# A second Strassen step in all seven products of layer 1's q and V

## The chip, the cores and the metric

The kernel runs on one core of one Trainium2 chip. The metric is the device time of one execution, in microseconds. The time before is 2786.17 us, the median of 3 runs (2785.94 to 2787.55).

A core has a TensorE (PE: matrix products, which it writes into PSUM), a VectorE (DVE), a ScalarE (ACT), a GpSimd (POOL) and a SyncE (SP, which issues transfers). Each works through its own instructions in order and waits on semaphores for the others. In this kernel a tile of PSUM is two banks of 512 fp32 columns by 128 partitions.

## The reference

Eight images of 512 channels by 32 x 32 positions pass through two attention layers, in fp32.

```python
# layer 0, 8 heads
h = group_norm(x, norm_w, norm_b)                  # 32 groups
qkv = einsum('oc,bchw->bohw', qkv_w, h) + qkv_b    # q, k, v by head
attn = softmax(einsum('bhnd,bhmd->bhnm', q, k) / sqrt(64))
x = x + proj_w @ (attn v) + proj_b
# layer 1, one head, statistics over the whole image
n = (x - mean(x)) * rsqrt(var(x) + eps) * gn_gamma + gn_beta
q, k, v = wq n + bq, wk n + bk, wv n + bv
attn = softmax(einsum('bci,bcj->bij', q, k) * 512 ** -0.5)
out = x + wo (einsum('bcj,bij->bci', v, attn)) + bo
```

## The kernel before

Layer 1's products are folded once, ahead of the images: q becomes one product with wq and wk together, whose partner in the scores is the image itself, and V one product with wv and wo together. The images are then worked on one after another. For image b the program runs layer 0's scores and values (`layer0`), then for image b+1, ahead of time, layer 0's V, its even pairs of heads (`qk02`), for image b the projection, for image b+1 the odd pairs (`qk13`), and then layer 1 of image b (`attention1`): q, V, scores, values.

**Strassen.** A product of 512 x 512 by 512 x 1024 is cut into quarters and computed as seven products of quarters instead of eight (the Winograd form): A11 B11, A12 B21, S1 T1, S2 T2, S3 T3, S4 B22 and A22 T4, where S1 to S4 are sums of quarters of A, and T1 to T4 of B. Some of these seven are cut again in the same way, which is called "twice" in the names. `pair` in `by_two_steps` (L614) does two such products side by side, in seven steps: both products' results share one bank, the left and the right half. Four of the seven products get the second step before the change (`PAIRS`); A11 B11, S2 T2 and S3 T3 (the "line") do not, in q, in V and elsewhere.

**q** (`make_q`, L1518) runs 12 products of 512 columns and 28 of 256. **V** (`make_v_twice`, L972) runs 56 of 128 columns and 24 of 256. ACT copies a sum that comes first into its place, DVE adds the later ones.

**Second-step operands.** What the second step needs is prepared: for the weights, sums of their quarters are made once, kept in DRAM, and fetched for each image on ACT's queue (`WeightTwice`, L556). For the image, `Ready.halve` makes them on GpSimd during `qk13` (`quarters_b`, L545; its instructions are at L535 and L541), four parts: B21, B22, T1, T4.

**Order.** PE's, ACT's and DVE's instructions stay in the order in which the program emits them. A product is a generator that yields after each step, and `at_steps` (L680) calls the hooks listed for a step's number between its steps, so a dictionary such as `hooks_v` says what DVE, ACT and GpSimd are given where. `together` (L668) interleaves generators. GpSimd's and SP's instructions are placed by the framework's scheduler.

**Buffers.** There are 36 SBUF tiles of 128 x 1024 in the pool "t", three weight tiles in "w", and in PSUM two tiles each of the tags "s" and "o" (two banks each, eight banks in all). A tile is taken over by the next request of its tag, which waits until everything that used it is done.

**Statistics.** Layer 1's mean and variance come from sums that ACT makes (`moments`, L335, two passes per 128 x 512 piece), which small GpSimd operations join (L350 to L356). A matmul with `in_sample` (L305) averages over the partitions and puts its result into the unused second bank of a product's PSUM tile (the list `spares`), DVE reduces it (L307), and then GpSimd (L363 to L367) and a second such matmul do the variance. Layer 0's statistics of image b+2 are made by the same means during image b's V: the image is loaded again for it, at q's step 3, in four pieces of 512 KB.

**q's combinations.** S1 to S4 of q for the scores (`finish_q`, by `finish`, L187; instructions at L195) and the second step's sums of S1 (`halve_a`, L518) are DVE work between V's steps.

**Kept.** The odd pairs' q and k go to DRAM after `qk13` (`Kept`, L921) and are fetched during layer 1's values; the even pairs' stay in SBUF.

## Time and profile before

| | |
|---|---|
| median of 3 runs | 2786.17 us |
| the profiled execution | 2786.2 us |
| its span | 2784.5 us |
| PE busy | 2777.8 us (100%) |
| DVE busy | 2117.3 us (76%) |
| ACT busy | 1178.1 us (42%) |
| GpSimd busy | 500.9 us (18%) |
| DMA, HBM over the span | 106 GB/s |

The span is that of the instructions on the core; the execution's own time is 1.7 us longer. Busy shares are of the span. A line of the timeline has the start in microseconds from the span's start, the length, the engine, the line of the kernel, the operation, output and input by the program's names, the shape, how many instructions in a row it stands for, and in brackets the idle time before and what ended it. PE's matmuls are pipelined, so the length of a group includes its last one's drain; the distance from start to start tells the pace.

### The profile page before, as it was taken

The numbers are of one execution on the slowest core, as the hardware profiler recorded it, in microseconds if no ns is written. First come the engines' busy times: TensorE is split into PE (matmuls) and PEld (weight loads), VectorE is DVE, ScalarE is ACT, GpSimd is POOL, SyncE is SP. The second block draws the span as 40 slices with busy tenths as digits, with TensorE's granted clock in tenths as the row PEclk, the third lists the DMA queues.
The fourth block names the chain that finished last, engine by engine and source line by source line (L and its number), as shares of the span: only waits on it lengthen the run. The fifth ranks groups of instructions, "written<-read, shape, count | busy, mean of one in ns | idle before, by whom it ended". The sixth has DMA issues, their size and how long they took to land.

```text
span 2784.5 us, 41074 instructions
## 1 busy us (share of the span) xinstructions
PE 2777.8 (100%) x16192; PEld 1620.0 (58%) x16192; DVE 2117.3 (76%) x2929; ACT 1178.1 (42%) x1883; POOL 500.9 (18%) x535
## 2 busy tenths in 40 slices
PE   9999999999999999999999999999999999999999
PEld 5437664377643776447764477645676356753375
DVE  6787677876788767887678775877758877688877
ACT  3462433625346153462525524265342643226622
POOL 0001240012400124002140031400413004220121
PEclk9999999999999999999999999999999999999999
DMA  7545513254132541325313253222533235131001
GB/s 258 193 119 171 185 57 111 58 182 170 57 110 58 185 168 65 107 62 201 144 65 107 77 201 129 89 90 74 196 129 110 69 102 197 69 140 32 23 16 39
DMA packets 103433, 321.32 MB, mean 115 GB/s; under 512 B 23820, under 2 KB 24620, under 8 KB 96832
## 3 DMA queue, kind: packets, MB, share of 16 engines
q1 hardware_dynamic: 81072, 268.75, 28.6%
q10 hardware_dynamic: 22160, 49.87, 5.4%
q8 instruction: 129, 2.11, 0.3%
q14 instruction: 72, 0.59, 0.1%
HBM read 231.01 MB, written 63.74 MB: 106 GB/s over the span
## 4 chain that ended last, share of the span: by engine, by line
PE 99%; DVE 0%; ACT 0%; issue 0%; POOL 0%; ACTq 0%; POOLq 0%
PE ps_o L1110 16%; PE s L1061 16%; PE ps_o L1867 10%; PE ps_l_v L708 6%; PE ps_l_qk L959 5%; PE ps_l L1701 5%; PE ps_s L1684 4%; PE ps_s_v L980 4%; PE ps_s L1701 4%; PE ps_s_qk L952 3%; PE ps_l_q L693 3%; PE ps_o_v L980 3%; PE ps_o_qk L952 3%; PE ps_l_p L693 3%; PE ps_s_q L1540 2%; PE ps_f_q L1540 2%
## 5 line engine op out<-in xcount | busy, mean ns | idle before, releaser
L865 ACT ACTIVATE p<-s 128x1024 f32<-128x1024 f32 x505 | 516.7, 1025 | 308.6 <-PE s L1061 301.4
L867 DVE TENSOR_TENSOR acc<-acc,p 128x1024 f32<-128x1024 f32 x384 | 469.0, 1221 | 63.4 <-ACT p L865 55.0
L1110 PE MATMUL ps_o<-p,v_back 64*64 64x512 f32 x3528 | 455.3, 589 | 0.0
L1110 PEld LDWEIGHTS ps_o<-p,v_back 64*64 64x64 f32 x3528 | 134.9, 133 | 243.6 <-issue 240.1
L1061 PE MATMUL s<-qk_back,qk_back 64*64 64x512 f32 x1792 | 233.0, 590 | 0.0
L1061 PE MATMUL s<-c_q,c_k 64*64 64x512 f32 x1736 | 224.4, 590 | 0.0
L535 POOL TENSOR_TENSOR B_twice_p<-o 128x512 f32<-128x512 f32 x14 | 20.9, 1494 | 1065.6 <-DMA kept_v<-c_v 607.9
L1867 PE MATMUL ps_o<-t_p,s_v 128*128 128x512 f32 x384 | 169.6, 596 | 0.0
L1061 PEld LDWEIGHTS s<-qk_back,qk_back 64*64 64x64 f32 x1792 | 67.7, 133 | 126.3 <-issue 113.0
L1061 PEld LDWEIGHTS s<-c_q,c_k 64*64 64x64 f32 x1736 | 64.9, 133 | 119.3 <-issue 103.2
L1675 ACT ACTIVATE p<-p,factor 128x512 f32<-128x512 f32 (+1 forms) x112 | 84.6, 780 | 114.8 <-DVE p L1711 87.9
L1867 PEld LDWEIGHTS ps_o<-t_p,s_v 128*128 128x128 f32 x384 | 71.8, 190 | 88.4 <-issue 88.0
L1711 DVE TENSOR_TENSOR p<-ps_l,p 128x512 f32<-128x512 f32 x136 | 90.8, 686 | 41.0 <-PE ps_l L1701 39.7
L644 DVE TENSOR_TENSOR c_v<-ps_l_v,c_v 128x512 f32<-128x512 f32 x120 | 80.0, 688 | 54.6 <-PE ps_l_v L708 54.4
L1689 ACT COPY p<-ps_s 128x512 f32<-128x512 f32 x96 | 53.1, 588 | 141.5 <-PE ps_s L1684 141.5
L867 DVE TENSOR_TENSOR acc<-p,p 128x1024 f32<-128x1024 f32 x57 | 69.7, 1222 | 47.8 <-ACT p L865 47.7
L1711 DVE TENSOR_TENSOR p<-ps_s,p 128x512 f32<-128x512 f32 x112 | 74.8, 685 | 36.6 <-PE ps_s L1701 21.7
L959 PE MATMUL ps_l_qk<-t,w_qk 128*128 128x512 f32 x224 | 98.4, 592 | 0.0
L626 ACT COPY c_q<-ps_s_qk 128x512 f32<-128x512 f32 x56 | 32.7, 584 | 138.8 <-PE ps_s_qk L952 138.8
L626 ACT COPY c_v<-ps_s_v 128x512 f32<-128x512 f32 x90 | 52.0, 585 | 86.8 <-PE ps_s_v L980 86.8
L535 POOL TENSOR_TENSOR B_twice<-x 128x512 f32<-128x512 f32 x16 | 20.1, 1277 | 373.7 <-PE ps_s_qk L952 196.6
L1672 POOL TENSOR_TENSOR acc<-acc,p 128x512 f32<-128x512 f32 x48 | 83.6, 1741 | 13.6 <-ACT p L1675 11.1
(579 smaller groups left out, 5703.7 us busy)
## 6 DMA issues: line engine op xcount, KB each, us to landing
x<-in_x SPq DMA_DIRECT2D x88, 512.0 KB, 10.3
w_qk<-stored_qk SPq DMA_DIRECT2D x14, 1792.0 KB, 9.2
fold<-acc SPq DMA_DIRECT2D x56, 256.0 KB, 4.0
qk_twice<-stored_qk_twice ACTq DMA_DIRECT2D x28, 512.0 KB, 3.9
kept_v<-c_v SPq DMA_DIRECT2D x28, 512.0 KB, 3.9
w_wqk<-stored_wqk SPq DMA_DIRECT2D x8, 1792.0 KB, 7.0
w_wvo<-stored_wvo SPq DMA_DIRECT2D x8, 1792.0 KB
v_back<-kept_v SPq DMA_DIRECT2D x28, 512.0 KB, 5.6
```

The lines of the kernel that those rows point to most:

```text
L693: nc.tensor.matmul(bank, w[a][:, k, c * P : (c + 1) * P], bs[b][:, k, :], start=fresh and k == 0, stop=k == 1, skip_group_check=True,)
L708: nc.tensor.matmul(bank[:, u * 2 * P : (u + 1) * 2 * P], bs[b][:, k, n * P : (n + 1) * P], w[a][:, k, :], start=fresh and u == k == 0, sto ...
L865: nc.scalar.activation(p, s, AF.Exp, scale=factor)
L867: nc.vector.tensor_tensor(acc, first, p, ALU.add)
L952: nc.tensor.matmul(bank[:, i * 2 * P : (i + 1) * 2 * P], parts[a][x], twice_b[v][y], start=start and i == 0, stop=True, skip_group_check=True,
L959: nc.tensor.matmul(bank, of(i, a)[:, k, :], bs[v][:, k, :], start=start and k == 0, stop=k == 1, skip_group_check=True,)
L980: nc.tensor.matmul(bank[:, (2 * i + u) * P : (2 * i + u + 1) * P], twice_b[v][y][:, u * P : (u + 1) * P], parts[a][x], start=start and i = ...
L1061: nc.tensor.matmul(s[cols, j, :], ks[pair][k0 // HALF][rows, k0 % HALF : k0 % HALF + HD], qs[pair][g][rows, :], start=True, stop=True,)
L1110: nc.tensor.matmul(o[cols, half, :], vs[n][kt % 4 // 2][rows, h, c0 : c0 + HD], p[rows, j, :], start=kt == 0, stop=kt == NT - 1,)
L1701: nc.tensor.matmul(bank[:, u * 2 * P : (u + 1) * 2 * P], v[y][:, u * P : (u + 1) * P], a[x], start=start and u == 0, stop=True, skip_group ...
L1711: nc.vector.tensor_tensor(at(r, t), bank, at(r, t), ALU.add)
L1867: nc.tensor.matmul(bank, v_parts[kt // 2][a][:, kt % 2, c * P : (c + 1) * P], p_parts[kt // 2][b][:, kt % 2, cols], start=fresh and kt == ...
```

## The change

It applies to images 0 to 6; the last image keeps the former q and V.

1. q and V: all seven products take the second step, in `seven_by_two_steps`. The groups z (A11 B11 and S2 T2, two products a step) and w (S3 T3) run interleaved first; then c (S1 T1 and A22 T4) and d (A12 B21 and S4 B22). d adds its results onto z, all by DVE. After z and w, four additions on DVE combine them; after c's last step (`n == 11`) four more are written, and after those d's last two. q needs 49 products of 256 columns, V 98 of 128.
2. The twice-combined weights of q and V grow from two tiles to four (the last half filled). The new sums are made once, by GpSimd, during image 0's round.
3. `Ready.halve` makes seven parts instead of four on GpSimd during `qk13`: 21 operations instead of 12.
4. The averages of layer 1's norm use the spare bank of z's "o" tile.
5. q's S1 to S4 and S1's second-step sums go from DVE to GpSimd, all at V's step 0. `Norm.untaken` makes one more small vector, `c_up`.
6. The even pairs' q and k are kept in DRAM too, and fetched at the values' step 6.
7. The second load of x is written in two parts, and its eight moments are divided: four in q's steps 15 to 24, four in V's.

```diff
+    REST = [[("A11", "B11"), ("S2", "T2")], [("S3", "T3")]]
+    TWICE = {"wqk1": PAIRS + REST, "wvo1": PAIRS + REST}
+        def __init__(self, name):
+            self.pairs, self.tiles = TWICE.get(name, PAIRS), []
+            for n, pair in enumerate(self.pairs):
+                t = flat(tile2(f"{name}_twice_{n}"))[:, : len(pair) * HALF]
+                nc.scalar.dma_start(t, stored[f"{name}_twice"][:, n * N : n * N + t.shape[1]])
+                self.tiles.append(t)
...
+    def seven_by_two_steps(multiply, at, z, c, w, bias, name):
+        def group(tag, products, use_of):
+            line, single = (banks(t, f"ps_{t}{tag}_{name}") for t in "so")
+            spares.append(single[:, 1, :])
+            line, single = line[:, 0, :], single[:, 0, :]
+            for bank, x, y, start, fresh, r, t in [
+                (line, "A11", "B11", True, True, 0, 0), (single, "A12", "B21", True, False, 0, 0),
+                (line, "S2", "T2", False, True, 0, 1), (single, "S1", "T1", True, True, 1, 1),
+                (line, "S3", "T3", False, False, 1, 1), (single, "S4", "B22", False, False, 0, 1),
+                (line, "A22", "T4", False, True, 1, 0),
+            ]:
+                multiply(bank, products, x, y, start)
+                tiles, always = use_of
+                to = at(tiles, r, t)
+                of = bank[:, : len(products) * 2 * P].rearrange("p (i q) -> p i q", i=to.shape[1])
+                if fresh and not always:
+                    nc.scalar.copy(to, of)
+                else:
+                    nc.vector.tensor_tensor(to, of, to, ALU.add)
+                yield
+        def plus(to, x, y, by=None):
+            if by is None:
+                nc.vector.tensor_tensor(to, x, y, ALU.add)
+            else:
+                nc.vector.scalar_tensor_tensor(to, x, by, y, ALU.add, ALU.add)
+        yield from together(group("z", REST[0], (z, False)), group("w", REST[1], (w, False)))
+        for k in range(2):
+            plus(z[k][:, 1, :], z[k][:, 0, :], z[k][:, 1, :], bias and bias(k, 0))
+        for k in range(2):
+            plus(w[k], w[k], z[k][:, 1, :], bias and bias(k, 1))
+        one = group("c", [("S1", "T1"), ("A22", "T4")], (c, False))
+        two = group("d", [("A12", "B21"), ("S4", "B22")], (z, True))
+        spares.clear()
+        next(one)
+        yield
+        n = 0
+        for g in [one, two] * 6 + [two]:
+            next(g)
+            n += 1
+            if n == 11:
+                for k in [1, 0]:
+                    plus(z[k][:, 1, :], z[k][:, 1, :], c[k][:, 0, :])
+                    plus(c[k], c[k], w[k].unsqueeze(1).to_broadcast([P, 2, HALF]))
+            if n < 13:
+                yield
+        if bias:
+            for k in range(2):
+                nc.scalar.activation(z[k][:, 0, :], z[k][:, 0, :], AF.Identity, bias=bias(k, 0))
+        yield
+        spares.clear()
...
+        if b == 0:
+            steps = [s for name in ["wqk1", "wvo1"] for s in make_twice(name, range(2, 4), None, nc.gpsimd)]
...
-        put_qk(pairs, 0, to["qs"], to["ks"])
+        to["qk02"] = Kept(pairs, f"qk02_{b % 2}")
-        for n, part in [(1, "B21"), (1, "B22"), (2, "T1"), (8, "T4")]:
+        for n, part in [(1, "B11"), (1, "B21"), (4, "T2"), (6, "T3"), (8, "B22"), (8, "T1"), (8, "T4")]:
             hooks.setdefault(n, []).append(lambda part=part: ready.halve(part))
...
+            hooks = {
+                1: [norm.both_halves], 5: [norm.mean_of_all], 8: [norm.deviation], 12: [norm.untaken],
+                16: [lambda: twice_w.append(WeightTwice("wvo1"))],
+            }
+                hooks[0], hooks[10] = ([lambda i=i: load_later(i)] for i in range(2))
+                for n in range(4):
+                    hooks.setdefault(15 + 3 * n, []).append(lambda n=n: measure_later(n))
+                    hooks_v.setdefault(15 + 3 * n, []).append(lambda n=n: measure_later(n + 4))
+            at_steps(make_q_twice(w), hooks)
...
-        for n in range(1, 5):
-            hooks_v.setdefault(2 * n + 3, []).append(lambda n=n: finish_q(n))
-        hooks_v.setdefault(17 if last else 13, []).append(lambda: halve_a("S1"))
+            for n in range(1, 5):
+                hooks_v.setdefault(0, []).append(lambda n=n: finish_q(n, nc.gpsimd))
+            hooks_v[0].append(lambda: halve_a("S1", None, nc.gpsimd))
+            at_steps(make_v_all(w), hooks_v)
...
-                    10: [lambda: put_qk(to["qk"].back(), 1, qs, ks)],
+                    6: [lambda: put_qk(to["qk02"].back(), 0, qs, ks)],
+                    10: [lambda: put_qk(to["qk13"].back(), 1, qs, ks)],
```

`make_q_twice` and `make_v_all` supply the two products with `multiply`, one matmul of 256 columns per product and step in q and two of 128 in V, and with `at`, the place of a quarter's result. `Norm.untaken` gets `c_up`, the difference of two columns of `c`, as a bias for w.

## The prediction

> **What bounds the kernel now.** First the page: busy time by engine, then the chain that ended last.

> ```profile
> PE 2777.8 (100%) x16192; PEld 1620.0 (58%) x16192; DVE 2117.3 (76%) x2929; ACT 1178.1 (42%) x1883; POOL 500.9 (18%) x535
> ...
> PE 99%; DVE 0%; ACT 0%; issue 0%; POOL 0%; ACTq 0%; POOLq 0%
> ```

> TensorE never rests, so a product less is worth its whole time, and any new wait of TensorE costs its whole length: nothing is slack on PE. The other engines matter only where PE would wait for them. Next the timeline of PE around one image's q and V (image 2):

> ```profile
> 995.65 1.93 PE L693 MATMUL ps_l_q<-x,w_wqk 128*128 128x512 f32 x4
> 997.42 1.89 PE L1540 MATMUL ps_f_q<-x,w_wqk 128*128 128x256 f32 x8
> ...
> 1018.87 0.61 PE L980 MATMUL ps_s_v<-w_wvo,x 128*128 128x128 f32 x4
> 1019.32 0.61 PE L980 MATMUL ps_s_v<-w_wvo,t 128*128 128x128 f32 x4
> ...
> 1034.94 7.17 PE L708 MATMUL ps_l_v<-w_wvo,t 128*128 128x256 f32 x32
> 1041.95 1.88 PE L1684 MATMUL ps_s<-q,x 128*128 128x512 f32 x4
> ```

> q takes 1018.87 - 995.65 = 23.22 us, V 1041.95 - 1018.87 = 23.08. A matmul shows as two records. From start to start, one of 512 columns paces at 0.8625 us, of 256 at 0.4313 ((999.15 - 997.42)/4, 999.15 being the next group's start), of 128 at 0.2234 (0.447 for four records).

> Then ACT, DVE and GpSimd in the same stretch, since they empty PSUM and feed the averages:

> ```profile
> 1019.96 0.59 ACT L626 COPY c_v<-ps_s_v 128x512 f32<-128x512 f32 x1 [2.02 <-PE ps_s_v L980]
> 1021.34 0.63 ACT L333 ACTIVATE mean<-x 128x512 f32<-128x512 f32 x1
> ```
> ```profile
> 976.59 1.88 DVE L440 TENSOR_TENSOR t<-x,x 128x1024 f32<-128x1024 f32 x1
> 1006.31 0.69 DVE L1528 TENSOR_TENSOR c_q<-ps_f_q,c_q 128x512 f32<-128x512 f32 x1 [0.17 <-PE ps_f_q L1540]
> 1023.31 1.22 DVE L195 TENSOR_TENSOR s_q<-q,q 128x1024 f32<-128x1024 f32 x1
> 1033.60 0.69 DVE L649 TENSOR_TENSOR c_v<-c_v,c_v 128x512 f32<-128x512 f32 x1
> ```
> ```profile
> 974.88 2.51 POOL L535 TENSOR_TENSOR B_twice<-x 128x512 f32<-128x512 f32 x2 [28.09 <-PE ps_s_qk L952]
> 977.34 6.86 POOL L541 TENSOR_TENSOR B_twice<-x,B_twice 128x256 f32<-128x256 f32 x4
> 990.66 0.20 POOL L350 TENSOR_TENSOR part<-part,stat 128x4 f32<-128x4 f32 x1
> 1007.18 0.30 POOL L363 TENSOR_SCALAR spread<-stat,mean_m 128x4 f32<-128x4 f32 x1 [14.92 <-DVE mean_m L307]
> ```

> A copy out of PSUM starts about 0.2 us after its matmul's paced end and holds ACT 0.59 us; a DVE add from PSUM takes 0.69 (0.60 apart when back to back); an SBUF add of 1024 columns 1.22 (1.13 apart), of 512 0.69. GpSimd's 12 halving operations end at 990.66, far ahead of the mean.

> [...] the 1024-column add is 1.88 us at 976.59, beside GpSimd, and 1.22 alone. [...]

> **The change, part by part**, for each of the seven images that get it.

> *Products.* q before: 12 x 0.8625 + 28 x 0.4313 = 22.42. After: all seven products in seven parts each, 49 x 0.4313 = 21.13. V before: 56 x 0.2234 + 24 x 0.4313 = 22.86; after 98 x 0.2234 = 21.89. Gain on paper 1.29 + 0.97 = 2.26; against the measured stages, which hold 0.28 of averages and about 0.7 of small gaps, up to 3.0.

> *The seam from q to V.* Call E the end of q's first half (groups z, w). Then c and d run 14 pairs of matmuls x 0.8625 = 12.08. In DVE's written order, four additions (`n == 11`) stand before d's last two adds, and the first needs ACT's copy of c's last sum: PE ends it at E + 12 x 0.8625 = E+10.35, the copy runs E+10.55 to 11.15. Then DVE: 0.73 + 1.13 + 0.73 + 1.13 (512, 1024, 512, 1024 columns; each 1024 one waits for the one before), then 0.60 and 0.69: E+16.1. d's last bank is the very bank that V's second product (group w) takes. PE gets there after V's first product, 4 x 0.2234 = 0.89, at E+12.97. So PE waits 16.1 - 12.97 = **3.1 us**. Behind it in PE's order stand all of V's other products; nothing covers it. Before, V's groups of four records follow one another at 0.447 us without a gap. Bounds: 2.6 (each DVE operation at its back-to-back pitch, no gap) to 3.9 (ACT's copy late by 0.8, below).

> *Averages.* The mean's and variance's sums move to the spare half of z's own tile, and the next z product waits for DVE's reduction: about 0.3 us to its start plus 0.15, less the pace: 0.4 each, **0.83** in all. Bounds 0.4 to 1.0.

> *GpSimd's halves.* 21 operations during the previous product instead of 12, ahead of the mean's small chain in GpSimd's order. Before: 990.66 - 974.88 = 15.8 for 12. After: three more parts of one 512- and two 256-column operations. By B21's pace (6.86/4 = 1.7 each, contended) and T's (1.0 each) about 2.8 to 4.7 per part; one can run before 974.88. So the chain ends at 998.3 to 1000.0, and PE arrives at 995.65 + 9 x 0.4313 = 999.5. Take **0.2**, bounds 0 to 1.5.

> q after: 21.13 + 0.28 + 0.83 + 0.2 = 22.44, so -0.8. V after: 21.89 + 3.1 = 25.0, so **+1.9**.

> *The seam from V to the scores.* The same order: c5, d4, then the four additions, d5, d6. V's first two additions need only DVE's work, so they start at its E'+10.7; 0.7 + 1.15 + 0.7 + 1.15 + 0.6 + 0.7 lead to E'+15.8 alone. The second score product takes d's bank and is due at E' + 14 x 0.8936 + 2.58 = E'+15.1. GpSimd begins S4's and A22's halves here, with contention on the four additions. Take **+1.0**, bounds 0.4 to 1.5.

> *Moved work.* q's S1 to S4 and S1's halves leave DVE (4 x 1.22 + 4 x 0.42 = 6.5) for GpSimd: 8 x 1.27 + 4 x 0.73 = 13.1 us from about E+16, done near E+30, before the scores at about E+38. They are hidden by V; uncovered they would cost up to 13. They can contend with DVE's four additions after V's first half, some tenths at most.

> *x's statistics.* Four of eight moments (0.63 + 0.19 + 0.72 + 0.19, 1.61 apart) move from V into q's c and d. ACT is then nearly full there: 4 x 1.61 + 3 x 0.59 = 8.2 in E+1.5 to E+10.6. If x lands 2 us late, c's last copy slips by about 0.8: the upper bound of the first seam.

> *DMA.* Per image 4 x 0.5 MB out and back for the even pairs, and 2 x 0.75 MB more of twice-combined weights: 5.5 MB. The page shows 106 GB/s over the span, but the stretch 996 to 1014 is dense. The even pairs leave at about 952 and are fetched during the values, at about 1107 against a first use near 1130. The page's last part has a load of this size, `v_back`, at 5.6 us from issue to landing. Cost 0, hidden by the values; uncovered, about 6 us. The extra weights queue on ACT behind landings that come before their use: 0.

> *Image 0.* 24 small GpSimd operations and four stores under V0: at most 1 us once, taken as 0.

> Sum: -0.8 + 1.9 + 1.0 = +2.1 us per image, x 7 = +15. The profiled execution took 2786.2 (span 2784.5, 1.7 around it), the median 2786.17: the same, so the forecast is **2801**. Ends: q -1.4, V +1.3, scores +0.4 make +0.3 per image (2788); q +0.9, V +2.7, scores +1.5 make +5.1 (2822).

> **Rivals.** (A) *The gain arrives*: DVE empties d's bank before V asks, or the wait falls elsewhere. For: PE is the bound and 2.26 to 3.0 us of products go. Against: DVE's order is written out, and 5.0 us of its work must fit between E+11.15 and E+12.97. With no seam cost, -2.7 x 7: 2767. It decides where the seam into V costs under 1.0 us with the other terms as taken (-0.8 - 1.2 + 1.0 + s < 0). (B) *GpSimd and ACT late too*: the mean held by the halves, copies held behind moments of a late x; +4 per image: 2814. For: contended 1.7 us GpSimd operations at 977. Against: ACT waits little there before. (C) *Stalls eat just the gain*: about 2787. (D) *The transfers bind*: the first score waits for the even pairs, 1 to 6 us per image, 2808 to 2843; against it the 20 us of cover above. That the order isn't what the diff says is excluded by the built order of PE, ACT and DVE.

> **How the numbers follow.** A change under 0.2% (5.6 us) can't be told from none. Forecast (2792 to 2808) 0.50; B 0.17; C 0.16; A 0.13; D 0.04. Faster: A, 0.13. Same: C, 0.16. Slower: the rest, 0.71. The range leaves out A's better part and D's: 2781 to 2822.

> **What would show it.** Right: V's second product starts 2.6 to 3.9 us after its first ends, its wait released by DVE's last add of q; two gaps of 0.4 us at the averages; a wait of 0.4 to 1.5 us before the second score product; q near 22.4 us and V near 25.0. Wrong: V at 22 us (A), or the mean's product waiting over 1 us for GpSimd, or PE waiting for ACT's copies in c and d (B), or the first layer-0 score waiting for a DMA (D).

## The result, and the profile after

The changed kernel takes 2852.8 us (median of 4 runs, 2847.12 to 2859.13) against 2786.86 before (4 runs): a ratio of 1.0237, 95% interval 1.0215 to 1.0259, so slower by 66 us. The forecast was slower by 15, with an upper end of 2822. The direction was right, the size was not.

The page's first lines and its chain, after:

```profile
span 2851.7 us, 42440 instructions
...
PE 2790.8 (98%) x16570; PEld 1665.5 (58%) x16570; DVE 2185.8 (77%) x2997; ACT 1193.4 (42%) x1939; POOL 674.6 (24%) x706
...
PE 25%; DVE 1%; issue 0%; ACT 0%; DVEq 0%
```

TensorE is busy 13 us *longer* although it has less to multiply, and it now stands still for about 60 us. The chain no longer helps, for the profile follows it over only about a quarter of the span. PE's waits do:

```profile
PE ps_sw_v L1782 <- DVE z_q L705: 21.7, 7, 3.1
PE ps_s L1839 <- DVE z_v L705: 14.1, 7, 2.0
PE ps_l_v L784 <- DVE c_v L659: 9.4, 1, 9.4
PE ps_oz_q L1700 <- DVE mean_m L307: 1.8, 7, 0.3
PE ps_oz_q L1700 <- DVE mean_v L307: 1.8, 7, 0.3
PE ps_sc_q L1700 <- ACT z_q L703: 1.7, 7, 0.2
PE ps_sc_v L1782 <- ACT z_v L703: 1.6, 7, 0.2
```

The columns are who waits, for whom, the sum in us, how often, and the longest. The first is the seam from q to V, to the tenth as forecast (3.1, seven times). The second is the seam into the scores, twice as long as forecast. The third comes once, in image 0's round. Together with the small ones these are 52 us, and they don't explain why PE is busy for longer. The timeline of PE behind the first wait (image 2) does:

```profile
1045.10 0.61 PE L1782 MATMUL ps_sz_v<-w_wvo,x 128*128 128x128 f32 x4
1045.55 0.61 PE L1782 MATMUL ps_sz_v<-w_wvo,t 128*128 128x128 f32 x4
1049.27 0.71 PE L1782 MATMUL ps_sw_v<-w_wvo,t 128*128 128x128 f32 x4 [3.11 <-DVE z_q L705]
1049.82 1.00 PE L1782 MATMUL ps_oz_v<-w_wvo,x 128*128 128x128 f32 x4
1050.61 1.06 PE L1782 MATMUL ps_oz_v<-w_wvo,t 128*128 128x128 f32 x4
1051.46 1.06 PE L1782 MATMUL ps_ow_v<-w_wvo,t 128*128 128x128 f32 x4
```

Ahead of the wait a group of four records follows the last one at 0.45 us; behind it the starts lie 0.79 and 0.85 us apart. Each stretch's clock and transfers, in the same place (columns: stretch, its length, busy time of PE, PEld, DVE, ACT and POOL with numbers of instructions, PE's granted clock, DMA share, GB/s):

```profile
1049.00:1050.00 1.00, 0.73 (x6) 0.73 (x7) 0.98 (x2) 1.00 (x3) 1.00 (x2) 0.94 1.04 444
1051.00:1052.00 1.00, 1.00 (x7) 1.00 (x6) 0.96 (x2) 0.00 (x0) 1.00 (x2) 0.50 0.28 115
1054.00:1056.00 2.00, 2.00 (x20) 2.00 (x19) 0.00 (x0) 1.57 (x4) 2.00 (x2) 1.00 0.00 0
```

The granted clock falls to 0.50 for 3.4 us once PE has stood for 3.1, and then comes back. From 1049.27 to 1053.68 six groups run that would take 6 x 0.447 = 2.68 us: 1.73 us more. In two images (the fifth and the seventh) the slow stretch is 6.8 us long and V takes 28.6 to 28.7; in one (the sixth) the clock holds behind the same wait, and V takes 26.9. So V is over its forecast of 25.0 without any change of clock; what the sixth image shows in its place is a wait for z's first V sum:

```profile
2099.10 0.71 PE L1782 MATMUL ps_sw_v<-w_wvo,t 128*128 128x128 f32 x4 [3.11 <-DVE z_q L705]
2102.93 0.71 PE L1782 MATMUL ps_oz_v<-wvo_twice,B_twice 128*128 128x128 f32 x4 [0.43 <-DVE z_v L705]
```

By starts, against the pace of 0.447, that V loses 3.4 us at the seam, 0.7 at this sum, 0.5 at c's start (ACT's copy of z's last sum) and 0.4 at a later c product: 5.0. Image 2 loses 3.4, 1.6 to the clock, and 0.5 at c: slow products hide the two waits on DVE. Net of that the clock costs V 0.5 us in four images and 1.8 in two.

By stages, from PE's starts (us; image 2 except where it says otherwise):

| stage | before | after | forecast |
|---|---|---|---|
| product `qk13` | 22.51 | 22.82 | 22.51 |
| q | 23.22 | 23.19 | 22.44 |
| V | 23.08 | 27.38 | 25.0 |
| scores and values | 88.64 | 90.72 | 89.6 |
| V ahead of image 1, once | 24.20 | 36.53 | 24.2 |

Over seven images V is 31.8 us longer, scores and values 19.9 (2.1 in four images, 3.7 to 4.1 in three), `qk13` 2.1, q 0.1; the one V is 12.3. That is 66.2 of the span's 67.2; of the rest, 0.6 lies ahead of image 1's V and 0.3 in layer 0's V of the later images.

The four runs differ by 12 us, and their mean granted clock differs with them: 0.994, 0.992, 0.991 and 0.990 at 2847.12, 2852.12, 2853.48 and 2859.13 us.

### The profile page after: what moved, and what is told of

Read it like the earlier page. It is cut to its first block, busy times and chain, and to the rows that moved or that the text cites. A ratio compares the mean times of both kernels' runs of the same rounds, so it can differ in the third digit from the quotient of the medians.

```text
span 2851.7 us, 42440 instructions
## 1 busy us (share of the span) xinstructions
PE 2790.8 (98%) x16570; PEld 1665.5 (58%) x16570; DVE 2185.8 (77%) x2997; ACT 1193.4 (42%) x1939; POOL 674.6 (24%) x706
## 5 line engine op out<-in xcount | busy, mean ns | idle before, releaser
L941 ACT ACTIVATE p<-s 128x1024 f32<-128x1024 f32 x505 | 516.5, 1024 | 308.5 <-PE s L1137 301.4
L1137 PE MATMUL s<-qk_back,qk_back 64*64 64x512 f32 x3528 | 457.5, 590 | 0.0
L1137 PEld LDWEIGHTS s<-qk_back,qk_back 64*64 64x64 f32 x3528 | 132.6, 133 | 245.5 <-issue 216.4
L2021 PEld LDWEIGHTS ps_o<-t_p,s_v 128*128 128x128 f32 x384 | 71.9, 190 | 88.4 <-issue 87.7
L537 POOL TENSOR_TENSOR B_twice<-x 128x512 f32<-128x512 f32 x23 | 35.6, 1548 | 358.7 <-DVE x L1446 177.2
L373 POOL TENSOR_TENSOR rstd<-rstd,minus_half 128x4 f32<-128x4 f32 (+1 forms) x16 | 12.9, 806 | 281.1 <-DVE rstd L372 281.1
L1035 PEld LDWEIGHTS ps_l_qk<-t,w_qk 128*128 128x128 f32 x224 | 42.0, 190 | 56.3 <-issue 50.2
L1839 PE MATMUL ps_s<-z_q,x 128*128 128x512 f32 x112 | 57.2, 636 | 14.1 <-DVE z_v L705 14.1
L659 DVE TENSOR_TENSOR c_v<-ps_l_v,c_v 128x512 f32<-128x512 f32 x64 | 42.6, 688 | 32.3 <-PE ps_l_v L784 32.2
```

What stands on the lines that cost most here:

```text
L537: engine.tensor_tensor(t[:, 0:4:2, :], part[:, :, 2 * P :], part[:, 0, :].rearrange("p (n q) -> p n q", n=2), ALU.subtract,)
L941: nc.scalar.activation(p, s, AF.Exp, scale=factor)
L1035: nc.tensor.matmul(bank, of(i, a)[:, k, :], bs[v][:, k, :], start=start and k == 0, stop=k == 1, skip_group_check=True,)
L1137: nc.tensor.matmul(s[cols, j, :], ks[pair][k0 // HALF][rows, k0 % HALF : k0 % HALF + HD], qs[pair][g][rows, :], start=True, stop=True,)
L1839: nc.tensor.matmul(bank, bs[v][:, k, t * P : (t + 1) * P], of[a][k], start=a == "A11" and k == 0, stop=k == 1, skip_group_check=True,)
L2021: nc.tensor.matmul(bank, v_parts[kt // 2][a][:, kt % 2, c * P : (c + 1) * P], p_parts[kt // 2][b][:, kt % 2, cols], start=fresh and kt == ...
```

## The experiments

Each edit is made to the changed kernel (2852.8 us) unless another is named. Times of the kernel before, beside each group: 2786.4 to 2787.2.

**Filling the wait.** Is it really the clock? 13 products of a constant with itself into an unused bank keep TensorE at work where it waits; nothing reads them.

```diff
+            filled = line[:, 1, :P]
...
                 multiply(bank, products, x, y, start)
+                if tag == "z" and bias is None and x == "A11":
+                    for _ in range(13):
+                        nc.tensor.matmul(filled, ones, ones, start=True, stop=True)
```

> The changed kernel, with 13 products of a constant 128 x 128 tile (2.9 us) written into an unused bank behind V's first product: they do nothing for the result and stand where TensorE waits anyway. Clock theory: the wait's end doesn't move (DVE sets it), but TensorE isn't idle, so the clock stays at 1.0: V 27.4 to 25.6 us in a middle image, seven images together about 15 us, 2837 us. Rival (late operands or banks behind the wait): no change, 2852 us; or the filling delays the work, 2860 us.

Measured 2846.5 us (2845.98 to 2848.32), 6.3 less. Its timeline:

```profile
1046.68 3.07 PE L702 MATMUL ps_sz_v<-ones 128*128 128x128 f32 x26
1049.94 0.71 PE L1786 MATMUL ps_sw_v<-w_wvo,t 128*128 128x128 f32 x4 [0.20 <-DVE z_q L709]
1050.49 0.61 PE L1786 MATMUL ps_oz_v<-w_wvo,x 128*128 128x128 f32 x4
1050.94 0.61 PE L1786 MATMUL ps_oz_v<-w_wvo,t 128*128 128x128 f32 x4
```

Work added, time gained. The times alone leave some doubt, for one of the changed kernel's runs took 2847.12; the traces decide: the same products now follow at 0.45 us in all seven images. Late operands or banks would have left them slow. The clock is shown as the cause of the slow products. The gain is less than half of the 15 expected: V takes 26.9 us in every image, as in the one whose clock held before, for the waits on DVE that the slow products had hidden appear. Of V's seven images 4 x 0.5 + 2 x 1.8 = 5.6 us was to be had, and V is 5.5 shorter. The scores are 1.7 us shorter too, for there the clock fell in two images instead of three; that is chance, for nothing was changed there.

**The additions after d's last adds.** The forecast put the seam down to DVE's order. In q alone:

```diff
-            if n == 11:
+            if n == (13 if bias else 11):
```

> Only q's four additions are written after d's last two adds; V's stay where they are. The changed kernel is the base (2852.8 us). Theory (order on DVE plus TensorE's granted clock): d's last bank is free 0.9 us after its product, so V's second product waits under 0.5 us instead of 3.1, TensorE's clock stays at 1.0 in V, and what is left is a wait of at most 1.4 us where V's own adds queue behind the four additions: V of a middle image 27.4 to about 23.5, so about 2852.8 - 7 x 3.7 = 2827 us, and a bit less where the clock also recovers in the scores. Rival (the slow records after the wait are operands or banks that come late, not the clock): they stay, V about 25.5, 2840 us. The wait of 2.0 us at the second score product stays under both.

Measured 2872.5 us (2871.85 to 2872.76): 20 us slower, the greatest miss. PE's waits of this run:

```profile
PE ps_oz_v L1782 <- DVE z_v L705: 32.9, 7, 5.0
PE ps_s L1839 <- DVE z_v L705: 14.1, 7, 2.0
```

The wait at V's second product is gone, as expected, but a longer one stands six steps into V, where V's z sum queues behind the additions. DVE there, in this run:

```profile
1057.57 2.17 DVE L710 TENSOR_TENSOR c_q<-c_q,w_q 128x1024 f32<-128x1024 f32 x1
1059.67 0.14 DVE L400 TENSOR_TENSOR both<-mean_m,rstd 128x1 f32<-128x1 f32 x1
1059.85 1.26 DVE L401 TENSOR_SCALAR bias<-v_g,both 128x4 f32<-128x4 f32 x1
1061.14 1.18 DVE L402 TENSOR_TENSOR bias<-v_b,bias 128x4 f32<-128x4 f32 x1
1062.24 0.68 DVE L705 TENSOR_TENSOR z_v<-ps_oz_v,z_v 128x512 f32<-128x512 f32 x1
```

Two operations on four columns take 1.2 us each, and the last addition 2.17 instead of 1.22: GpSimd has just begun on q's combinations. The sum from PSUM keeps its 0.68.

The same for q and V:

```diff
-            if n == 11:
+            if n == 13:
```

> The four additions come after d's last two adds in q and in V. As for q alone, and the wait at the second score product (2.0 us, seven times, with slow clock behind it in three images, 5 us in all) is gone: about 19 us less than with q alone, 2808 us. Rival (that wait is GpSimd's contention, not the order): 1 us of it stays per image, 2815 us.

2860.1 us (2859.14 to 2862.06): the wait at the second score product is gone, but one of 1.6 us comes 11 us into the scores, where their sums queue on DVE behind the additions and what these delayed. Against q alone, 12 us less; 19 were expected.

**GpSimd later, or the tiny operations earlier.** Two tests of the contention, both on top of q's additions last. One asked for GpSimd's work at V's step 12:

```diff
-                hooks_v.setdefault(0, []).append(lambda n=n: finish_q(n, nc.gpsimd))
+                hooks_v.setdefault(12, []).append(lambda n=n: finish_q(n, nc.gpsimd))
```

> As the run with q's four additions last (2872.5 us), and q's combinations are given to GpSimd at V's step 12 instead of step 0. There V's fifth wait, 4.65 us for z's first V sum, had in front of it on DVE the four additions and three tiny operations of the norm's bias, each of which took 1.2 us beside GpSimd. Theory (GpSimd holds DVE up): the bias operations take 0.2 us each and the fourth addition 1.2 instead of 2.2, the wait falls from 4.65 to about 1.7 us, too short for the clock to fall, V from 29.9 to about 24.6: 2835 us. Rival (the four additions alone make the wait): it stays above 3.5 us and the clock still falls, 2862 us or more.

2871.2 us, but this one tells nothing: GpSimd's order is the scheduler's, the step only says where the instruction is written, and nothing made it wait. The trace shows the combinations right where they were. The other took the three bias operations at q's step 13:

```diff
+            hooks.setdefault(13, []).append(lambda: biases.append(norm.bias()))
             at_steps(make_q_twice(w), hooks)
-        bias = norm.bias()
+        bias = norm.bias() if last else biases[0]
```

> As the run with q's four additions last (2872.5 us), with the three tiny bias operations of the norm taken at q's step 13 instead of between q and V. If GpSimd holds these up beside its combinations (2.6 us of the wait of 4.65), the wait falls to about 2.1 us and in most images the clock holds: 2840 to 2850 us. If the four additions make the wait, it stays above 4 us, 2868 us.

2846.3 us (2845.88 to 2847.99), 26 less than with the additions alone: the wait is 2.07 us, where it was 4.65. So the three tiny operations, which take 0.15 to 0.23 us each where they stand now, made 2.6 us of it, seven times, about 2.0 of them GpSimd's hold. The clock didn't hold: in five of seven images it fell behind the shorter wait too. Of the gain, 20 us lie in V; 7 lie in the scores, where the clock fell in none of seven images instead of four, which is chance again.

**Image 0.** The timeline of SyncE's queue after, at the wait of 9.4 us:

```profile
245.09 2.08 SPq L611 DMA_DIRECT2D stored_wvo_twice<-wvo_twice  x2
247.27 0.59 SPq L1330 DMA_DIRECT2D few<-sums  x1
249.90 0.31 SPq L1336 DMA_DIRECT2D inv_rows<-few  x1
```

`few<-sums` gathers the softmax sums and is asked for at 235.21 before, at 247.27 after. It stands behind stores that wait for GpSimd's new sums. DVE's reciprocal waits for it, and behind that the sum that frees PE's bank. First the ten steps were moved to the even pairs:

> The changed kernel, with image 0's new sums of weights moved from the steps of V for image 1 to those of the even pairs after it. Theory (the small transfer of the softmax sums stands on SyncE's queue behind stores that wait for GpSimd): that V goes from 36.5 us to 24.2, 12 us less in all, 2840 us. Rival (GpSimd's work itself slows DVE there): half of it moves along into the even pairs, 2847 us.

2852.5 us, nothing won: V fell to 24.24, 12.3 less, and the even pairs rose from 22.39 to 41.76, 19.4 more. (The time is nearly the same because the clock by chance cost the scores 3.7 and V 2.3 us less.) ACT stood there at the fetch of the projection's weights, into a tile that a sum on GpSimd freed, with PE's copies behind it. Then to the second half of image 0's layer 0, where neither is due:

```diff
+            for n, step in enumerate(steps):
+                at_units.setdefault(42 + 2 * n, []).append(step)
...
```

> The changed kernel, with image 0's new sums of weights on GpSimd during the second half of image 0's layer 0 scores, where neither a softmax sum nor ACT's transfers wait behind them. Theory (the 12 us of image 0 are queues that stand behind these sums, on SyncE first, on ACT when moved to the even pairs): V for image 1 takes 24.2 us and nothing else grows, 2840 us. Rival (the SBUF tiles that these sums take make something else wait wherever they are): 2850 us or more.

2836.6 us (2836.43 to 2842.31), 16 less. That V is 24.55, and layer 0 is longer by 1.0: 11 of the 16. The rest is the clock, down in fewer images in the scores (3.7 us) and for shorter in V (2.6); that part is chance and not what the move is worth.

**Both seams cleared.** The additions are held back and given to DVE later, q's one at V's step 0 and three at step 3, V's in the scores' steps 9 to 12:

```diff
+            for n in reversed((0, 3, 3, 3)):
+                hooks_v.setdefault(n, []).insert(0, lambda: later_q.pop(0)())
...
+            for n in (9, 10, 11, 12):
+                hooks.setdefault(n, []).append(lambda: later_v.pop(0)())
```

> The changed kernel with both sets of four additions taken off the seams: q's first one at V's step 0 and three at V's step 3, V's at the scores' steps 9 to 12, and q's combinations to GpSimd after them (step 4). Theory: no wait over 0.5 us at either seam, TensorE's clock 1.0 from image 0's layer 1 on, V about 22.9 us (27.4 to 28.7 before this), scores and values 2.1 us shorter and 1.7 more in three images: 2852.8 - 33 - 14 - 5 = about 2800 us. Rival (DVE and GpSimd together have too much to do in V, wherever it stands): waits of 1 to 3 us at other places, 2820 us or more.

2812.3 us (2811.47 to 2812.6), 40 less. Its waits, first two lines:

```profile
PE ps_oc_v L1782 <- DVE c_v L705: 11.4, 7, 1.6
PE ps_l_v L784 <- DVE c_v L659: 9.4, 1, 9.4
```

Both seams are gone, and scores and values take 88.4 us, 0.2 less than before. In V a wait of 1.6 us is left, behind four additions of V's own which GpSimd's combinations now meet; the clock stays at 1.0 there. V is 24.6 where 22.9 was expected, which is the 12 us by which the whole misses its forecast.

**Towards a faster kernel.** With the sums in layer 0 too, and q's w ahead of z, so that the averages take w's bank:

```diff
-        yield from together(group("z", REST[0], (z, False)), group("w", REST[1], (w, False)))
+        first = [group("z", REST[0], (z, False)), group("w", REST[1], (w, False))]
+        yield from together(*(first[::-1] if bias else first))
```

> The additions spread, image 0's sums in layer 0, and q's group w ahead of z, so that the averages use w's bank, which is not needed again so soon, and z's last copy has more time before c. Theory: the sum of the parts, 2800 - 12 - 7 x 1.4 = 2778 us, 0.3% under the kernel before. Rival (the second step in all products gains nothing even without the seams): 2786 us or more.

2800.0 us, 22 more than expected. V's wait of 1.6 us is still there, and q differs from image to image: the last image of the seven, which has no x to measure, has q in 22.06, the others 22.4 to 24.2, with waits for ACT's copies of up to 1.7 us. Was it x, or the fetch of V's weights on ACT's queue? All moments go to V:

```diff
-                    hooks.setdefault(15 + 3 * n, []).append(lambda n=n: measure_later(n))
-                    hooks_v.setdefault(15 + 3 * n, []).append(lambda n=n: measure_later(n + 4))
+                for n, at in enumerate((2, 5, 8, 11, 15, 18, 21, 24)):
+                    hooks_v.setdefault(at, []).append(lambda n=n: measure_later(n))
```

> The run with the additions spread, sums in layer 0 and w ahead of z (2800.0 us), with x's eight moments all in V. If it was the late x that held ACT's copies in q's c: q 22.1 to 22.5 us in all images and no wait for ACT there, 2794 us. If it was the fetch of V's weights on ACT's queue: the waits stay, 2799 us.

q is 22.06 throughout, with the fetch where it was. The move takes the moments' work out of q together with their wait for x; that x was late is to be seen in the trace of the run before it, where ACT stood for it in each of the six images, up to 2.5 us. But the run takes 2808.4 us, for V rises to 27.4: ACT and DVE are now crowded there, the wait at c is 2.35 us, and the clock falls again. The next splits V's first additions (two of them after c's and d's first adds), keeps the moments in V, fetches V's weights at step 20 and takes the mean at step 4:

```diff
+        joined(0)
...
+            if n == 2:
+                joined(1)
...
-                1: [norm.both_halves], 5: [norm.mean_of_all], 8: [norm.deviation], 12: [norm.untaken],
-                16: [lambda: twice_w.append(WeightTwice("wvo1"))],
+                1: [norm.both_halves], 4: [norm.mean_of_all], 8: [norm.deviation], 12: [norm.untaken],
+                20: [lambda: twice_w.append(WeightTwice("wvo1"))],
```

> The last run (2800.0 us) with what its trace still shows: of the four additions after V's first half, the two that c's first DVE add and d's first one don't need come after these; x's eight moments all stand in V again; the fetch of V's twice-combined weights is asked for at q's step 20 instead of 16, and the mean is taken one step earlier. Theory: the wait of 1.63 us at V's c is gone (11 us in all), ACT's copies in q's c aren't held by a late x or by the weights' fetch (6 us of waits, 9 us by the one image without them), the mean's wait of 0.25 us is gone (2 us): 2778 us, faster than the kernel before by 0.3%. Rival (ACT or DVE is simply full in V, so the waits move): 2788 us or more.

2787.0 us, ratio 1.0000 (0.9992 to 1.0008): as before, q 21.64 and V 24.38. What was left in V were 0.9 us for DVE beside GpSimd, and 0.7 for ACT's copy behind a moment. Last, GpSimd is made to wait by its operands: q's last two additions go to V's steps 14 and 16.

```diff
-            for n in reversed((0, 3, 3, 3)):
+            for n in reversed((0, 3, 14, 16)):
...
-                for n, at in enumerate((2, 5, 8, 11, 15, 18, 21, 24)):
+                for n, at in enumerate((3, 7, 8, 16, 18, 20, 22, 24)):
```

> The mended run (2787.0 us) with q's last two additions at V's steps 14 and 16, so that GpSimd's combinations of q, which need them, start after V's own first additions, and x's moments moved away from z's last copy. Theory (what is left in V is DVE held up by GpSimd, 0.9 us at d, and ACT's copy behind a moment, 0.5 us at c): V 24.4 to about 22.7 us, GpSimd is done some 2.5 us into the scores and nothing waits for it: 2775 us, 0.4% faster than the kernel before. Rival (GpSimd is late for the scores): V as said and a wait of 1 to 3 us in the scores, 2783 us or more.

2773.8 us (2773.31 to 2774.12), ratio to before 0.9953 (0.9939 to 0.9966): 0.47% faster than before and 79 us faster than the change as made. The page and PE's waits of it:

```profile
PE 2762.7 (100%) x16570; PEld 1649.8 (60%) x16570; DVE 2182.7 (79%) x2997; ACT 1197.1 (43%) x1939; POOL 688.7 (25%) x706
```
```profile
PE ps_sc_v L1784 <- ACT z_v L703: 1.6, 7, 0.2
PE ps_warm L2218 <- POOL in_sample L164: 1.2, 1, 1.2
PE s L1141 <- ACT p L945: 0.8, 1, 0.8
```

PE has the changed kernel's number of matmuls (16570) and 28 us less busy time. Of the waits left before, that of 0.9 us is gone and that of 0.7 is 0.2. GpSimd's timeline (image 2, V begins at 1015.15) shows that all but one of the combinations' operations now start in V's second half, behind DVE's addition:

```profile
1020.09 1.27 POOL L1774 TENSOR_TENSOR s_q<-z_q,c_q 128x512 f32<-128x512 f32 x1 [19.08 <-DVE c_q L710]
1031.29 1.28 POOL L1774 TENSOR_TENSOR s_q<-z_q,c_q 128x512 f32<-128x512 f32 x1 [9.94 <-DVE c_q L710]
```

q is 21.64 and V 22.53 us: 2.1 us per image under the kernel before, near the 2.26 that the products promised on paper.

## Why the prediction was right or wrong

**The step that failed** is the rule that the sum was made by: any new wait of TensorE costs its whole length. Each wait was priced alone, with nothing behind it, and one term, image 0, was put at nothing. The span grew by 67 us where the sum has 15. Of the 52 that it lacks, V has 18 (13 in smaller waits that the sum did not hold, 5.6 in clock), the scores 13 (7.5 in a longer wait, 5.4 in clock), image 0 has 12, q 6, `qk13` 2 and the rest 1.

**Products: right.** The gain of 2.26 us per image exists; the last run has 2.1 of it.

**The seam from q to V: the wait right, its price wrong.** The wait is 3.11 us where 3.1 was worked out, released by DVE as described; that it fits to the tenth is in part luck, for both of its ends came about 0.8 us later than written (c's late start, c's and d's small gaps), which cancels. V is 26.9 where the clock held, not 25.0: 0.7 for z's first V sum, queued on DVE behind d's adds and the bias operations that GpSimd holds up, 0.5 at c's start, 0.4 at c's second DVE sum, and 0.3 for PE's new start behind the seam. The prediction let GpSimd's moved work meet DVE only later, at V's own four additions and for some tenths; it met the bias operations first, which took 3.2 us together instead of 0.5. The clock adds 0.5 or 1.8 on top. The prediction looked at no rival of that kind, and the trace before shows nothing of it: PE's clock is 1.00 throughout there. In the changed kernel's trace the clock fell to 0.50 behind six of the seven waits of 3.1 us (for 3.4 us in four images, 6.8 in two) and behind three of the seven of 2.02; the numbers stand in the last section. In the whole run the clock cost about 13 us net: 5.6 in V, 5.4 in three images' scores, 1.7 behind the wait of 9.4.

**The seam into the scores: mechanism right, size off.** 2.02 us against 1.0 (bounds 0.4 to 1.5). The term is the four additions beside GpSimd: 1.74 and 1.63 for the two of 1024 columns and 1.21 for one of 512, after:

```profile
1071.46 1.74 DVE L710 TENSOR_TENSOR c_v<-c_v,w_v 128x1024 f32<-128x1024 f32 x1
1073.12 1.21 DVE L710 TENSOR_TENSOR z_v<-z_v,c_v 128x512 f32<-128x512 f32 x1
1074.36 1.63 DVE L710 TENSOR_TENSOR c_v<-c_v,w_v 128x1024 f32<-128x1024 f32 x1
```

That is 1.4 us over the same operations alone (1.22 and 0.69), and the sum had 0.3 for it. The trace before had the rows that price this (1.88, which the prediction shows, and 1.75 beside GpSimd, 1.22 alone). In three images the clock fell here as well, 1.7 to 2.0 us each, and there nothing hid it.

**Image 0: wrong.** "At most 1 us once" was 12.3. The step priced GpSimd's operations and not the stores behind them on SyncE's queue, ahead of the softmax sums' gather.

**q: wrong by 0.7.** The two averages cost about 1.1 (0.25 of wait each, and each start after a wait 0.1 more), not 0.83; c's start cost 0.4, which was not in the sum; c and d 0.25. GpSimd's halves were in time: its chain ended at 1024.6, PE arrived at 1025.8. That part of rival B is refuted; late x, its other part, is small here (ACT stood for it up to 1.4 us, PE behind that 0.4 once) and showed fully only once the larger waits were gone.

**`qk13`: 0.3 per image, unforeseen.** It is the same in every kernel that has seven halves on GpSimd there, the fastest too. DVE beside GpSimd is a guess; no run took it apart.

**Transfers: right.** No wait of PE for a kept pair; rival D falls. What no rival held is that a wait moves the next ones and the clock, and that a transfer of 16 KB can stand behind a store.

## What to carry to other kernels

A wait of the engine that never rests had two prices here: its length, and, where 2.015 us or more of it fell into one interval of the clock's grid (last section), products at a granted clock of 0.50 behind it, which in turn hid shorter waits; so short waits apart from each other can be cheaper than one long one, and taking the long one away shows the next. As the grid's place differed from run to run, compare the stages in the traces and not the times alone. When a scheduler orders an engine, a step written later is not done later: give it an operand that comes later. When work is moved, list for every instruction it issues, the stores too, which small, urgent one will stand behind it on its queue.

## What the runs showed of the hardware

How long TensorE stood, and whether its clock fell, from the traced runs (the wait, and in how many cases the granted clock was 0.50 behind it; the runs by the names of the experiments above):

| wait, us | clock fell | runs |
|---|---|---|
| 1.59 to 1.64 | 0 of 22 | additions last in both; spread; spread with sums in layer 0; moments in V |
| 2.02 | 15 of 49 | the change; additions last in q; filled; sums in the even pairs; sums in layer 0; GpSimd later; bias early |
| 2.07 | 5 of 7 | bias early |
| 2.33 to 2.35 | 5 of 6 | moments in V |
| 3.1 | 20 of 21 | the change; sums in the even pairs; sums in layer 0 |
| 4.65 to 5.0 | 21 of 21 | additions last in q; in both; GpSimd later |

```profile
1046.47:1049.88 3.41, 0.61 (x5) 1.00 0.90 328
1049.88:1053.30 3.42, 3.42 (x18) 0.50 0.43 184
2094.35:2097.77 3.42, 1.64 (x12) 1.00 0.50 113
2097.77:2101.18 3.41, 2.08 (x18) 1.00 0.98 416
2101.18:2104.59 3.41, 2.98 (x26) 1.00 0.05 16
```

In the third image 2.80 us of the wait fall into one interval, and the next one is slow. In the sixth the wait is cut into 1.78 and 1.33 us by the interval's edge, and the clock holds.

A DVE operation on four columns took 1.2 us beside GpSimd's 128 x 512 operations (1.18 and 1.26 in the run with q's additions last) and 0.16 to 0.23 alone (with the bias early). The 1.26 is a `TENSOR_SCALAR`, with one tensor operand in SBUF and a column of scalars there; the 1.18 is a `TENSOR_TENSOR`, with two tensor operands. DVE's sums from PSUM into 128 x 512 took at most 0.69 us, beside GpSimd too (269 of them in the changed kernel's trace).
